# Moving sums, activation steps and prologue pieces in a four-layer state-space kernel

## The chip, the cores and the metric

The kernel runs on one core of a Trainium2 chip, as one program. The metric is its device time in microseconds (us), the median of several runs. All data are float32.

## The reference

Input x is 4 images of 64 x 64 positions (L = 4096) with 128 channels. Layers 0, 1 and 3 are selective state-space blocks, layer 2 is a gated block. Cut to what matters, a state-space block computes, for each of K = 4 directions (rows, columns, and both reversed), DI = 256 channels and N = 16 states:

```python
x_dbl = einsum('bkdl,kcd->bkcl', xs, x_proj_w)          # 8 + 16 + 16 rows
dts, Bs, Cs = split(x_dbl, [R, R + N], axis=2)
delta = softplus(einsum('bkrl,kdr->bkdl', dts, dt_w) + dt_b)
def step(h, t):                                          # over L positions
    x_t, d_t, B_t, C_t = t
    h = exp(d_t[..., None] * A) * h + (d_t * x_t)[..., None] * B_t[:, :, None, :]
    return h, einsum('bkdn,bkn->bkd', h, C_t)
```

Ahead of it stand a layer norm, a projection, a depthwise 3 x 3 convolution and Silu; behind it the four directions are summed, normed, multiplied by Silu of a second projection z, projected and added to the input, and an MLP with Gelu follows.

## The kernel before, in words

**Turns, chunks, periods.** A turn is one state-space layer of one image: 12 turns (`turns`), the images two by two, so that the work between two layers of one image can lie beside the other image's scans. A turn has 32 chunks: four directions by eight chunks of 512 positions. A chunk has 8 periods i = 0 to 7; each handles 4 of the 16 states for one half (128) of the channels. There are 3072 periods. The order of every engine's instructions is written out by hand in the loop over periods (L935 and after); each engine runs its own list in that order, and waits are set by a framework from the tiles.

**A period.** `scan` (L864) is one VectorE scan over 512 positions. Its decay factors `da` come from ScalarE (`decay`, L849: two Exp per call, two calls, made one period ahead). For two of the four states ("side 0") the driving term comes from TensorE in one PSUM tile `dbp` (`pair_db`, L841, issued one period ahead, right after the two scans that free the tile); for the other two ("side 1") VectorE multiplies `dup`, a PSUM copy of delta times x made by ScalarE (`lift`, L857), with `bb`, rows of B that a DMA has spread over the partitions: product `dbv` (L984), one PSUM tile. `lift` copies only in periods 7, 0, 2, 4 and 6, where the half changes. GpSimd multiplies each pair of states with rows of C (`times_c`, L880, tile `hc`); in periods 0, 2, 4, 6 (`PAIRED`) it also adds the two sides. TensorE sums over states by products with the identity into PSUM (`add_up`, L886, tile `yp`): per period two calls for a paired period, four for another. VectorE adds finished sums to `y_sb` (`leave`, L905). `diagonals` (L831) builds on ScalarE the diagonal matrices for `pair_db`; `save` (L874) keeps the last state; `spread` (L816) issues the DMAs of `bb` and `cb` on SyncE's queue.

**The order in a period of before.** ScalarE: decay of the next period, side 0; save; then decay side 1, save, `lift`, `diagonals`. TensorE: the two calls of side 0 of the period before, if that was not paired; `pair_db` for the next period; at the end the two calls of side 1 of the period before. VectorE: two scans, product, scan, product, scan, then in periods 0 and 1 a `leave`.

**Pieces.** The next chunk's preparation is a generator, `prologue` (L761): fetch x; project it to the 40 rows [dt; B; C] (or, for a reversed direction, fetch the rows that the forward one has stored); delta of both halves by projection and Softplus; transposed B (`bt`); `du` = delta times x on GpSimd; `du` transposed (`duT`). `piece(number)` (L945) goes on to its next `yield` at the numbers in `PIECES`; number 2i is behind `pair_db` in period i, 2i + 1 near the period's end. The Softplus piece holds two table loads[...].

**Steps of the work between layers.** Everything else (norms, projections, convolution, Silu, MLP, Gelu) is a list of small steps that `between` makes. `other(number)` (L950) has four slots in each period (0 between the first two scans, 1 behind `piece(2i)`, 2 behind the third scan, 3 at the end) and takes steps from the list's head as their share of the turn has come. `rest` puts empty steps between; `later` sets stores back. The `run` step of `silu` (L419) and `gelu` (L484) are one long activation each, 1024 or 2048 columns, with a table load on either side. In `silu`, `turn` (L424) copies the result transposed into the tile `down` and `store` writes that out; `down` lies in the buffers "cen" and "sq", which `norm` uses too.

**Buffers.** [...] two banks for dbp, one each for dbv, dup, two yp, `misc` (all of the prologue) and `gap` (all the steps). `h` and `hc` have four buffers, `da` three.

Of the kernel before, what the change touches and what calls it, by code (L numbers as in the profile page):

```python
# [13 lines left out]
F32 = mybir.dt.float32  # L14
AF = mybir.ActivationFunctionType
# [10 lines left out]
CH = 512  # L26
NCH = L // CH
RPC = CH // W
P = 128
# [4 lines left out]
PAIRED = (0, 2, 4, 6)  # L34


PIECES = (0, 3, 4, 6, 8, 9, 10, 11, 12, 13)


_VSS = [  # L40
# [24 lines left out]
def vss_stack_kernel(ctx: ExitStack, tc: tile.TileContext, x: bass.AP, weights, out: bass.AP, n_batch=B, layers=(0, 1, 2, 3)):  # L65
# [86 lines left out]
    gap1 = ctx.enter_context(tc.tile_pool(name="gap1", bufs=1))  # L152
    gap2 = ctx.enter_context(tc.tile_pool(name="gap2", bufs=2))
    gap3 = ctx.enter_context(tc.tile_pool(name="gap3", bufs=3))

    def combine(i, psums):

# [39 lines left out]
    def between(e, frm, to, psums):  # L197
# [219 lines left out]
        def silu(c, of_z):  # L417

            def run():  # L419
                part = z.wide[:, 0 if of_z else 2 : 2 if c is None else 4]  # L420
                nc.scalar.activation(part, part, AF.Silu)
# [43 lines left out]
        def mlp(c, store):  # L465
            def fresh():
                z.t = gap1.tile([P, CH], F32, tag="t", name="t")
                return z.t

            norm(lambda: z.res, fresh, v["n2w"], v["n2b"], eps5)  # L470
            for j in range(4):

                def up(j=j):
                    if j == 0:
                        z.wide = gap1.tile([P, 4, CH], F32, tag="wide", name="hid")
                    z.ps = bank()
# [279 lines left out]
    def scans(pool, ring, deep, psum):  # L756
# [4 lines left out]
        def prologue(s):  # L761
# [5 lines left out]
            if s.first:  # L767
                s.dt = pool.tile([R, DI], F32, tag="dt", name="dt_w")
                nc.sync.dma_start(out=s.dt, in_=weights[s.layer][1][:, s.k * DI : (s.k + 1) * DI])
            yield  # L770


            s.xd_d = lane.xd[s.k % 2][s.c]
            s.xd = pool.tile([2 * NX, CH], F32, tag="xd", name="xd")
            if s.back:
                nc.sync.dma_start(out=s.xd[:NX], in_=s.xd_d[1])
                yield
            else:
# [3 lines left out]
                yield  # L782
# [3 lines left out]
            for m in halves:  # L786
                ps = psum.tile([P, CH], F32, tag="misc", name="ps_dt")
                nc.tensor.matmul(ps, s.dt[:, m * P : (m + 1) * P], s.xd[:R], start=True, stop=True)  # L788
                yield
                func = AF.Identity if m == halves[0] else AF.Softplus  # L790
                nc.scalar.activation(s.delta[:, m], ps, func, bias=v["dtb"][:, s.k, m : m + 1])  # L791
            m = halves[0]
            nc.scalar.activation(s.delta[:, m], s.delta[:, m], AF.Softplus)  # L793
            nc.scalar.preload_act_table_set("natural_log_exp_and_others")
            ps = psum.tile([P, 4, NX], F32, tag="misc", name="ps_bt")
            for j in range(4):
                nc.tensor.transpose(ps[:, j, :], s.xd[:NX, j * P : (j + 1) * P], ident[:NX, :NX])
# [66 lines left out]
        def scan(s, i, side, j, da, db):  # L864
            q, m = place(s, i)
            if j == 0:
                s.h[i, side] = deep.tile([P, 2, CH], F32, tag="h", name="h")
            n = CQ * q + 2 * side + j
            init = 0.0 if s.first else s.state[:, m, n : n + 1]
            nc.vector.tensor_tensor_scan(  # L870
                s.h[i, side][:, j, s.step], da[:, j, s.step], db[:, s.step], init, ALU.mult, ALU.add
            )
# [10 lines left out]
            if side == 1 and i in PAIRED:  # L883
                nc.gpsimd.tensor_add(hc, hc, s.hc[i, 0])  # L884

        def add_up(s, i, side):  # L886
            if side == 0 and i in PAIRED:
                return
            q, m = place(s, i)
            start, end = (0, 7) if m == s.flip else (1, 6)  # L890
            opens = i == start and side == int(i in PAIRED)
            if opens:
                setattr(s, f"yp{m}", psum.tile([P, CH], F32, tag=f"yp{m}", name="yp"))
            for j in range(2):
                nc.tensor.matmul(  # L895
                    getattr(s, f"yp{m}"),
                    ident,
                    s.hc[i, side][:, j],
                    start=opens and j == 0,
                    stop=i == end and side == 1 and j == 1,  # L900
                )
            if i == end and side == 1:
                full.append((s, m))

        def leave(s, m):  # L905
            yp, xs = getattr(s, f"yp{m}"), s.xs[:, m]
# [28 lines left out]
        for at, (s, i) in enumerate(periods):  # L935
# [14 lines left out]
            def other(number):  # L950

                gone = at % (8 * per_turn) * 4 + number
                for todo, count, frm, to in segments:
                    while todo and count - len(todo) < count * (gone - frm) / (to - frm):
                        todo.pop(0)()

            da_next = [None, None]
# [6 lines left out]
                save(*before, 1)  # L964
            if spreads:
                spread(*spreads, 0)
            scan(s, i, 0, 0, da[0], s.db[:, :, 0])
# [11 lines left out]
            if then:  # L979
                da_next[1] = decay(*then, 1)  # L980
            save(s, i, 0)
            for j in range(2):
                db = psum.tile([P, CH], F32, tag="dbv", name="dbv")
                nc.vector.tensor_mul(db, s.dup, s.bb[i // 2][:, j])  # L984
                scan(s, i, 1, j, da[1], db)
                if j == 0:
                    other(2)
            times_c(s, i, 1)
            if then:
                if then[1]:  # L990
# [5 lines left out]
                diagonals(s, q, half)  # L996
            elif nxt:
                diagonals(nxt, q - 4, half)
            if i < 2 and full:
                leave(*full.pop(0))  # L1000
            if before:
                add_up(*before, 1)
            piece(2 * i + 1)
            other(3)
            da = da_next
            before = (s, i)
            if then and then[0].turn != s.turn:
                assert not any(todo for todo, *_ in segments)
        save(*before, 1)
        add_up(*before, 0)  # L1010
        add_up(*before, 1)
        while full:
            leave(*full.pop(0))
        for todo, *_ in segments:
# [95 lines left out]
```

## Time and profile before

| what | us |
|---|---|
| median of 3 runs | 23305.67 (23292.7 to 23313.06) |
| the profiled execution, its own time | 23325.13 |
| its span, first to last instruction | 23323.4 |
| busy: VectorE / TensorE / GpSimd / ScalarE | 20362.5 / 20052.7 / 19260.3 / 18075.1 |
| first scan starts at | 165.58 |
| scans (12288) | mean 1.20 to 1.28 each |
| GpSimd products and sums of 128 x 1024 (7680) | 2.36 each |
| products dbv (6144) | 0.69 each |
| table loads | 1.28 each |

The profile is one execution. Its page gives the busy time of each engine, the idle time ahead of groups of instructions and who ended it; its lists of waits name the waiting instruction and line, then the releaser. PE is TensorE, PEld its weight loads, DVE is VectorE, ACT ScalarE, POOL GpSimd, SPq SyncE's queue. A line of a timeline is: start, duration, engine, line, operation, output<-inputs, shapes, count, and in brackets the idle time before it with its releaser. A period takes 7.59 us in the mean (23323.4 less the opening and the end, by 3072), but not the same in all turns: the turns with layer 2's work between (the fourth, fifth, tenth and eleventh) take 2027 to 2037 us, the others 1834 to 1907.

### The profile page before, as it was taken

To read this page: it belongs to the slowest core of one execution; us is meant where nothing else is said; L and a number is where in the kernel's file an instruction comes from. 1 tells how busy PE (TensorE), PEld (TensorE's weight loads), DVE (VectorE), ACT (ScalarE), POOL (GpSimd) and SP (SyncE) were. 2 spreads that over 40 slices of the span, in tenths; PEclk is the share of its full clock that TensorE was granted. 3 is DMA by queue.
4 is the path that set the end of the run, shared out by engine and by line. 5 is a ranking of instruction groups with operands and counts; after the bars stand their busy time and mean duration, and the time that the engine had idled before them with its cause. 6 is when DMAs were issued, how large, how long until landed. Compare 5 with 4: busy or idle time off the path is not lost. (4 is left out here: it accounts for less than half of the span.)

```text
span 23323.4 us, 216855 instructions
## 1 busy us (share of the span) xinstructions
PE 20052.7 (86%) x58234; PEld 10604.8 (45%) x58234; DVE 20362.5 (87%) x20186; ACT 18075.1 (77%) x38870; POOL 19260.3 (83%) x8862
## 2 busy tenths in 40 slices
PE   7888888888888888888888888888888888888887
PEld 3444444444444444444444444444444444444443
DVE  5999899988887888898899899898988878888996
ACT  5788787777777787787788787787877777877886
POOL 5898888888887787888888788888888878878885
PEclk8999999999999999999999999999999999999998
DMA  4444444444334434434533544444443443344332
GB/s 104 147 142 144 131 130 145 131 131 140 125 125 126 130 126 126 135 130 134 139 133 130 139 138 132 134 144 127 132 141 122 126 128 131 123 128 136 131 132 101
DMA packets 2437558, 3060.09 MB, mean 131 GB/s; under 512 B 1753840, under 2 KB 1790064, under 8 KB 2238192
## 3 DMA queue, kind: packets, MB, share of 16 engines
q1 hardware_dynamic: 2436336, 3046.22, 42.1%
q8 instruction: 472, 7.73, 0.1%
q14 instruction: 750, 6.14, 0.1%
HBM read 2784.41 MB, written 261.49 MB: 131 GB/s over the span
## 5 line engine op out<-in xcount | busy, mean ns | idle before, releaser
L882 POOL TENSOR_TENSOR hc<-h,cb 128x1024 f32<-128x1024 f32 x6144 | 14420.4, 2361 | 3675.8 <-DVE h L870 2362.9
L895 PE MATMUL yp<-hc,ident 128*128 128x512 f32 x18432 | 9087.0, 620 | 641.9 <-POOL hc L884 395.2
L854 ACT ACTIVATE da<-delta,w 128x512 f32<-128x512 f32 x12288 | 8158.8, 713 | 1557.2 <-DVE h L870 1532.3
L845 PE MATMUL dbp<-diag,duT 128*128 128x256 f32 x24576 | 6276.1, 400 | 1832.3 <-DVE h L870 1729.2
L870 DVE TENSOR_TENSOR_SCAN h<-da,state,dbp 128x512 f32<-128x512 f32 x5376 | 6564.8, 1259 | 939.5 <-PE dbp L845 757.6
L870 DVE TENSOR_TENSOR_SCAN h<-da,state,dbv 128x512 f32<-128x512 f32 x5376 | 6879.6, 1280 | 477.6 <-ACT da L854 11.1
L845 PEld LDWEIGHTS dbp<-diag,duT 128*128 128x128 f32 x24576 | 4740.1, 198 | 4329.2 <-issue 2850.9
L895 PEld LDWEIGHTS yp<-hc,ident 128*128 128x128 f32 x18432 | 3491.1, 198 | 4992.6 <-issue 3633.6
L984 DVE TENSOR_TENSOR dbv<-dup,bb 128x512 f32<-128x512 f32 x6144 | 4226.0, 688 | 614.2 <-ACT dup L862 400.7
L837 ACT ACTIVATE diag<-ident,bt 128x128 f32<-128x128 f32 x12288 | 3947.5, 401 | 0.2
L884 POOL TENSOR_TENSOR hc<-hc 128x1024 f32<-128x1024 f32 x1536 | 3622.5, 2358 | 120.4
L862 ACT COPY dup<-du 128x512 f32<-128x512 f32 x1920 | 1125.3, 586 | 1267.6 <-DVE dbv L984 1231.8
L402 PE MATMUL gap<-halo,cw 128*128 128x512 f32 x3456 | 1658.6, 605 | 15.6 <-ACT wide L413 6.2
L870 DVE TENSOR_TENSOR_SCAN h<-da,dbp 128x512 f32<-128x512 f32 x768 | 892.5, 1200 | 130.8 <-PE dbp L845 104.1
L870 DVE TENSOR_TENSOR_SCAN h<-da,dbv 128x512 f32<-128x512 f32 x768 | 937.3, 1220 | 79.3 <-ACT da L854 14.1
L805 POOL TENSOR_TENSOR du<-delta,xs 128x512 f32<-128x512 f32 x768 | 978.3, 1274 | 33.7 <-ACT delta L793 33.7
L788 PE MATMUL ps_dt<-xd,dt_w 8*128 8x512 f32 x1536 | 887.2, 658 | 124.9 <-ACT delta L791 73.6
L402 PEld LDWEIGHTS gap<-halo,cw 128*128 128x128 f32 x3456 | 642.1, 192 | 743.8 <-issue 700.7
L878 ACT COPY state<-h 128x2 f32<-128x2 f32 x5376 | 960.9, 179 | 0.0
L413 ACT ACTIVATE wide<-gap,w 128x512 f32<-128x512 f32 x192 | 132.1, 688 | 824.2 <-PE gap L402 824.1
L813 ACT COPY duT<-ps_duT 128x512 f32<-128x512 f32 x768 | 440.0, 573 | 181.3 <-PE ps_duT L811 180.5
L791 ACT ACTIVATE delta<-ps_dt,w 128x512 f32<-128x512 f32 x768 | 524.6, 683 | 37.2 <-PE ps_dt L788 32.6
(121 smaller groups left out, 11443.0 us busy)
## 6 DMA issues: line engine op xcount, KB each, us to landing
cb<-xd_d SPq DMA_DIRECT2D x1536, 1024.0 KB
bb<-xd_d SPq DMA_DIRECT2D x1536, 512.0 KB
xs<-x_row_d SPq DMA_DIRECT2D x192, 512.0 KB
xs<-x_col_d SPq DMA_DIRECT2D x192, 512.0 KB
x_col_d<-down SPq DMA_DIRECT2D x192, 256.0 KB
x_row_d<-wide SPq DMA_DIRECT2D x96, 512.0 KB
y_d<-y_sb SPq DMA_DIRECT2D x96, 512.0 KB
y<-y_d SPq DMA_DIRECT2D x96, 512.0 KB
```

Source lines behind the costliest of these rows:

```text
L402: nc.tensor.matmul(z.ps, z.cw[:, m, t, :], z.halo[c][:, dy : dy + RPC, dx : dx + W], start=(t == 0), stop=(t == 8),)
L805: nc.gpsimd.tensor_mul(s.du[:, m], s.delta[:, m], s.xs[:, m])
L837: nc.scalar.activation(s.diag[q][:, t, :, j], ident, AF.Copy, scale=s.bt[:, t, CQ * q + j : CQ * q + j + 1])
L845: nc.tensor.matmul(s.db[:, t * P : (t + 1) * P, :], s.duT[:, t, m, :], s.diag[q][:, t], start=True, stop=True)
L854: nc.scalar.activation(da[:, j], s.delta[:, m], AF.Exp, scale=s.v["a"][:, s.k, m, n : n + 1])
L862: nc.scalar.copy(s.dup, s.du[:, m])
L870: nc.vector.tensor_tensor_scan(s.h[i, side][:, j, s.step], da[:, j, s.step], db[:, s.step], init, ALU.mult, ALU.add)
L878: nc.scalar.copy(s.state[:, m, n : n + 2].unsqueeze(2), s.h[i, side][:, :, s.end : s.end + 1])
L882: nc.gpsimd.tensor_mul(hc, s.h[i, side], s.cb[i // 2][:, 2 * side : 2 * side + 2, :])
L884: nc.gpsimd.tensor_add(hc, hc, s.hc[i, 0])
L895: nc.tensor.matmul(getattr(s, f"yp{m}"), ident, s.hc[i, side][:, j], start=opens and j == 0, stop=i == end and side == 1 and j == 1,)
L984: nc.vector.tensor_mul(db, s.dup, s.bb[i // 2][:, j])
```

## The change

1. `PIECES` has 14 entries for 10, and the prologue's pieces are cut so that nearly each gives work to one engine. The rows of a reversed direction are fetched with x. B is transposed, and the rows stored, before the second half of delta. The Softplus piece runs at number 9, behind `lift` and `diagonals` of period 4, where it was at number 8, ahead of them; the `du` products run at 10 and 11 (9 and 10 before), the transposes at 12 and 13 (11 and 12), the last copy at 14 (13).
2. `add_up` takes a list of calls. An even period has three, those that are left of the odd period before; an odd one has the two of the paired period before and the first of its own. In odd periods they stand behind the last slot. None stands ahead of `pair_db` in its period any more.
3. `run` of `silu`, and `gelu`, are marked long. At the head of the list, a long step and all behind it are held until slot 3, and in period 4 until slot 3 of period 5.
4. The second product stands ahead of slot 2, not behind it. In period 1, `leave` stands between that product and its scan.
5. Ahead of the first layer, `down` has its own tile with two halves, in the buffer "y".

```diff
-PIECES = (0, 3, 4, 6, 8, 9, 10, 11, 12, 13)
+PIECES = (0, 2, 3, 4, 5, 6, 7, 8, 9, 10, 11, 12, 13, 14)
...
+    long = set()
...
-                z.down = gap1.tile([P, W, RPC], F32, tag=("cen", "sq")[m], name="down")
+                if frm is not None:
+                    z.down = gap1.tile([P, W, RPC], F32, tag=("cen", "sq")[m], name="down")
+                elif m == 0:
+                    z.downs = gap1.tile([P, 2, W, RPC], F32, tag="y", name="down")
+                if frm is None:
+                    z.down = z.downs[:, m]
...
+            long.add(run)
             S.append(run)
...
+            long.add(gelu)
             S.append(gelu)
...
             if s.back:
                 nc.sync.dma_start(out=s.xd[:NX], in_=s.xd_d[1])
-                yield
-            else:
+            yield
+            if not s.back:
                 ps = psum.tile([P, CH], F32, tag="misc", name="ps_x")
...
-                yield
+            yield
+            if not s.back:
                 nc.scalar.copy(s.xd, ps[: 2 * NX])
+            yield
...
+            project(halves[0])
+            yield
+            take(halves[0], AF.Identity)
+            yield
             ps = psum.tile([P, 4, NX], F32, tag="misc", name="ps_bt")
...
             nc.scalar.copy(s.bt, ps[:, :, R : R + N])
+            yield
+            project(halves[1])
+            yield
+            take(halves[1], AF.Softplus)
+            nc.scalar.activation(s.delta[:, halves[0]], s.delta[:, halves[0]], AF.Softplus)
+            nc.scalar.preload_act_table_set("natural_log_exp_and_others")
+            yield
             s.du = pool.tile([P, 2, CH], F32, tag="du", name="du")
...
-        def add_up(s, i, side):
-            if side == 0 and i in PAIRED:
-                return
+        def add_up(s, i, calls):
             q, m = place(s, i)
             start, end = (0, 7) if m == s.flip else (1, 6)
...
+            for call in calls:
+                opens = i == start and call == (2 if i in PAIRED else 0)
+                if opens:
+                    setattr(s, f"yp{m}", psum.tile([P, CH], F32, tag=f"yp{m}", name="yp"))
+                side, j = divmod(call, 2)
+                closes = i == end and call == 3
+                nc.tensor.matmul(getattr(s, f"yp{m}"), ident, s.hc[i, side][:, j], start=opens, stop=closes)
+                if closes:
+                    full.append((s, m))
...
                     while todo and count - len(todo) < count * (gone - frm) / (to - frm):
+                        if (number < 3 or i == 4) and todo[0] in long:
+                            break
                         todo.pop(0)()
...
-            if before:
-                add_up(*before, 0)
             if then:
                 pair_db(*then)
             piece(2 * i)
...
-            for j in range(2):
-                db = psum.tile([P, CH], F32, tag="dbv", name="dbv")
-                nc.vector.tensor_mul(db, s.dup, s.bb[i // 2][:, j])
-                scan(s, i, 1, j, da[1], db)
-                if j == 0:
-                    other(2)
+            scan(s, i, 1, 0, da[1], product(0))
+            db = product(1)
+            other(2)
+            if i == 1 and full:
+                leave(*full.pop(0))
+            scan(s, i, 1, 1, da[1], db)
...
-            if i < 2 and full:
+            if i == 0 and full:
                 leave(*full.pop(0))
-            if before:
-                add_up(*before, 1)
+            if i % 2 == 0 and before:
+                add_up(*before, (1, 2, 3))
             piece(2 * i + 1)
             other(3)
+            if i % 2:
+                add_up(*before, (2, 3))
+                add_up(s, i, (0,))
```

More of the change, by code (lines that the diff above doesn't have):

```diff
@@ L769, in prologue @@
                 nc.sync.dma_start(out=s.dt, in_=weights[s.layer][1][:, s.k * DI : (s.k + 1) * DI])
-            yield
+            ps = None
             s.xd_d = lane.xd[s.k % 2][s.c]
@@ L781, in prologue, with project, take @@
                     nc.tensor.matmul(ps[: 2 * NX], v["xp"][:, s.k % 2, m, :], s.xs[:, m], start=(m == 0), stop=(m == 1))
-                yield
+            yield
+            if not s.back:
                 nc.scalar.copy(s.xd, ps[: 2 * NX])
+            yield
             s.delta = pool.tile([P, 2, CH], F32, tag="delta", name="delta")
             halves = (s.flip, 1 - s.flip)
-            for m in halves:
+            def project(m):
+                nonlocal ps
                 ps = psum.tile([P, CH], F32, tag="misc", name="ps_dt")
                 nc.tensor.matmul(ps, s.dt[:, m * P : (m + 1) * P], s.xd[:R], start=True, stop=True)
-                yield
-                func = AF.Identity if m == halves[0] else AF.Softplus
+            def take(m, func):
                 nc.scalar.activation(s.delta[:, m], ps, func, bias=v["dtb"][:, s.k, m : m + 1])
-            m = halves[0]
-            nc.scalar.activation(s.delta[:, m], s.delta[:, m], AF.Softplus)
-            nc.scalar.preload_act_table_set("natural_log_exp_and_others")
+            project(halves[0])
+            yield
+            take(halves[0], AF.Identity)
+            yield
             ps = psum.tile([P, 4, NX], F32, tag="misc", name="ps_bt")
@@ L884, in times_c @@
                 nc.gpsimd.tensor_add(hc, hc, s.hc[i, 0])
-        def add_up(s, i, side):
-            if side == 0 and i in PAIRED:
-                return
+        def add_up(s, i, calls):
             q, m = place(s, i)
             start, end = (0, 7) if m == s.flip else (1, 6)
-            opens = i == start and side == int(i in PAIRED)
-            if opens:
-                setattr(s, f"yp{m}", psum.tile([P, CH], F32, tag=f"yp{m}", name="yp"))
-            for j in range(2):
[L895 to L903, printed above, removed]
+            for call in calls:
[7 more added lines that the diff above has]
+                    full.append((s, m))
         def leave(s, m):
@@ L966, in scans, with product @@
                 spread(*spreads, 0)
+            def product(j):
+                db = psum.tile([P, CH], F32, tag="dbv", name="dbv")
+                nc.vector.tensor_mul(db, s.dup, s.bb[i // 2][:, j])
+                return db
             scan(s, i, 0, 0, da[0], s.db[:, :, 0])
@@ L981, in scans @@
             save(s, i, 0)
-            for j in range(2):
-                db = psum.tile([P, CH], F32, tag="dbv", name="dbv")
-                nc.vector.tensor_mul(db, s.dup, s.bb[i // 2][:, j])
-                scan(s, i, 1, j, da[1], db)
-                if j == 0:
-                    other(2)
+            scan(s, i, 1, 0, da[1], product(0))
[4 more added lines that the diff above has]
+            scan(s, i, 1, 1, da[1], db)
             times_c(s, i, 1)
@@ L1009, in scans @@
         save(*before, 1)
-        add_up(*before, 0)
-        add_up(*before, 1)
+        add_up(*before, (1, 2, 3))
         while full:
```

## The prediction

> **What bounds the kernel now.** I read the page's engine shares first: VectorE 87%, TensorE 86%, GpSimd 83%, ScalarE 77% busy, no engine full. The scans are a serial chain on VectorE, and from the first scan (165.6 us) to the last period VectorE hardly stops, so I count what it waits for. This is the list of VectorE's waits: who waited, line, releaser, total us, times, longest.
>
> ```profile
> DVE h L870 <- PE dbp L845: 861.7, 417, 10.8
> DVE dbv L984 <- ACT dup L862: 400.7, 205, 5.5
> DVE cen L245 <- ACT gap L242: 262.2, 140, 10.7
> DVE h L870 <- ACT da L854: 131.0, 77, 17.1
> ...
> DVE cen L230 <- DMA x_col_d<-down: 65.1, 2, 32.6
> ```
>
> Two waits lead: a scan waiting for TensorE's product dbp (862 us) and the product dbv waiting for ScalarE's lift dup (401 us). I then sorted these waits in the trace by the period i (0 to 7) that they fall in, four scans being one period. dup: 69, 53, 0, 33, 0, 201, 0, 46 us. dbp: 20, 134, 34, 130, 105, 229, 67, 143: odd periods 636, even 226. Period 5 is worst in both. The timeline of ScalarE ahead of one dup wait in period 5 shows why:
>
> ```profile
> 2846.89 1.28 ACT L791 ACT_TABLE_LOAD   x1
> 2848.19 0.69 ACT L791 ACTIVATE delta<-ps_dt,w 128x512 f32<-128x512 f32 x1
> 2848.77 0.62 ACT L793 ACTIVATE delta<-delta 128x512 f32<-128x512 f32 x1
> 2849.41 1.28 ACT L794 ACT_TABLE_LOAD   x1
> ...
> 2852.14 1.28 ACT L421 ACT_TABLE_LOAD   x1
> 2853.44 1.91 ACT L421 ACTIVATE wide<-wide 128x2048 f32<-128x2048 f32 x1
> 2855.36 1.28 ACT L220 ACT_TABLE_LOAD   x1
> 2856.66 0.59 ACT L862 COPY dup<-du 128x512 f32<-128x512 f32 x1
> ```
>
> The Softplus block (3.87 us) and a Silu with its tables (4.47 us) both stand ahead of the 0.59 us lift. VectorE at that moment:
>
> ```profile
> 2857.28 0.70 DVE L984 TENSOR_TENSOR dbv<-dup,bb 128x512 f32<-128x512 f32 x1 [5.11 <-ACT dup L862]
> ```
>
> Third, TensorE ahead of an odd period: a late pair_db, with VectorE idle 2.46 us for it.
>
> ```profile
> 2622.14 1.88 PE L402 MATMUL gap<-halo,cw 128*128 128x512 f32 x4
> 2623.86 1.88 PE L895 MATMUL yp<-hc,ident 128*128 128x512 f32 x4
> 2625.58 1.89 PE L845 MATMUL dbp<-diag,duT 128*128 128x256 f32 x8
> 2627.60 2.45 DVE L870 TENSOR_TENSOR_SCAN h<-da,state,dbp 128x512 f32<-128x512 f32 x2 [2.46 <-PE dbp L845]
> ```
>
> [...] The trace has the 1283 ns (384 loads, 492.7 us); [...] loads follow their neighbours within 0.1 us, so I use the trace. [...] lift waits behind both tables. So an order is all that this change has to offer, and all that it can spoil.
>
> **The change part by part.** Instruction counts do not change on any engine; what changes is order. The sum is made against the profiled execution, span 23323.4 us in 23325.1 us; the median of the runs is 19.5 us lower.
>
> *Lifts.* After the change no Silu or Gelu is issued between the period's decays and its lift, and the Softplus block comes behind lift and diagonals in period 4, not ahead. I take 0.9 of 401 us: −360. In the 46 chunks with over 1 us of dup wait in period 5, periods 5 to 7 idle 7.4 us in sum, in the others 2.6; the difference, 4.8, exceeds the dup wait itself (4.0), so it isn't given back, and a further 46 × 0.7 us, diagonals queued behind the lift, goes too: −30. Bounds: −200 (period 5 alone) to −430. What is late next on ScalarE is decay: a lift can start about 5.1 us into a period (two scans 2.4, product 0.7, scan 1.28, product 0.7), lift and four diagonals end at 7.0, the Softplus block at 10.9, a Gelu at 11.5, and the next two decays (1.33) at 12.2 or 12.8. Their reader starts at 15.2 (two periods of 7.59). That leaves 3.0 and 2.4 us of cover; other steps' ScalarE work eats some of it, so I charge +30 (0 to +130, the size of today's da wait again).
>
> *Three calls a period.* A summing call is two instructions that issue 0.43 us apart: 0.86 us. Between the pair_db issued in an odd period and the one issued in an even period stand 4 calls today, on the other side 2; afterwards 3 and 3. I compared in the trace the end of each pair_db with the end of VectorE's work before the scan that needs it. Scans of odd periods miss by 696 us in sum; 0.86 us earlier, but never before the scan that frees dbp, gives 471. Scans of even periods miss by 223; 0.86 us later, less TensorE's idle time just before that pair_db, gives 383. Net −65. The one-engine pieces take the wait of TensorE on ScalarE out of its queue (ps_dt on delta 74 us, ps_bt on delta 58), but move a projection and a set of transposes (0.9 and 0.6 us) from odd to even sides: I charge +15 for the two together, so −50. The call that joins an odd period's own end waits for GpSimd's first hc of that period; behind it stand the next slot's steps and pair_db, and behind that the scan. In a late case of the timeline that hc started 6.2 us and ended 8.6 us into its period; pair_db cannot start before the second scan of the next, at 7.6 + 2.4 = 10.0, so 1.4 us cover it: 0. Bounds for the whole: −250 (odd side gains, even side pays nothing) to +200 (the reverse).
>
> *du, the product, leave.* GpSimd gets one du (1.27 us) in each half of period 5, none behind period 4's three big products. Waits of scans on du and hc are 28.7 and 12.6 us; of VectorE's other steps, a quarter now waits behind the second product, 0.7 us of cover each. I take −40 (0 to −80). leave in period 1 is the same 0.88 to 1.06 us of VectorE, earlier: 0. Cover: its yp was closed a period before; if it were late, one wait of today's size (7 us in all).
>
> *xd beside x, its store earlier.* Each of 192 fetches (80 KB) is issued with x, one 0.37 us slot on SyncE's queue ahead of the spreads. Those stand issued a median 17.8 (bb) and 14.4 us (cb) before their first reader: 0. If that cover were gone: 192 × 0.4 = 77 us.
>
> *down in its own buffer.* In the opening, VectorE and ScalarE wait twice for the store of down: the mean is done at 87.9 and its reader starts at 91.9 us, the square waits from 92.6 to 99.2. 2 × 10.6: −21. Its new buffer is y's, which nothing holds there by then.
>
> *What the held-back steps add.* A long step at the head of the list holds all behind it until the period's last slot, from period 4 even until that of 5, seven slots; then they go out together. Counted in the order of the built program: in 7 chunks at the end (last turn, period 5) Silu, gate, projection and VectorE's add share one slot. ScalarE ends about 0.7 us into the next period, GpSimd still has hc and du and reaches the end of gate at 6.0, TensorE's projection at 7, and VectorE stands for about 7.5 us: +52. For 11 Gelus in period 5 three or four of their `down` products are issued right behind, ahead of three summing calls and pair_db. Gelu ends 2.9 into the next period, 4 × 0.86 and 3 × 0.86 end at 8.9, pair_db at 10.9 instead of 7.6: 3.3 us each, 36; the first `down` comes in the same or the next slot for 54 more Gelus, at an estimated 0.3 us each: together +50. Gate and stores of x_col wait for a Silu closer behind them: +30. Bounds for all this: +60 to +400.
>
> Sum: −360 −30 +30 −50 −40 −21 +52 +50 +30 = −339. 23325.1 − 339 = 22986 for such an execution, 22967 at the median's level. I say **22965 us**.
>
> **The rivals.** *Nothing gained:* the dup wait turns into a da wait because ScalarE, 77% busy, is late either way. For it: da already costs 131 us. Against it: ScalarE itself idles 1532 us for buffers of da, so it runs ahead. Given back are, say, 340 of the 390 us: 22967 + 340 = 23307. *More gained:* the pieces and the third call relieve the odd sides by 1.46 us instead of 0.86 (call and transposes); odd misses then fall from 696 to about 355, and even ones stay at 223 because TensorE waits for buffers there (1535 us in sum ahead of even pair_dbs). That is −340 in place of −50: about 22675; half of it, 22820, is more likely. *Slower, by bursts:* 262 long steps are issued in the scans, 79 of them in period 5 with up to seven slots of others behind. Gains are 501 us in the sum; from 501/262 = 1.9 us a long step the change loses. At 2.3 us each: 262 × 2.3 − 501 = +100, 23405. For it: seven of them cost 7.5. Against it: most are followed by rests or by work that only ScalarE does. That the change doesn't do what it says is excluded: the built order shows no Silu or Gelu ahead of a lift, and three calls in every period.
>
> **How the numbers follow.** Forecast 0.60 (own range 22820 to 23120), more gained 0.18, nothing gained 0.10, slower 0.12. Differences under 0.2% (47 us) can't be told from none. The forecast and the larger gain are faster, 0.78; of nothing gained, nearly all is within 0.2%: 0.09; slower takes 0.13 with the rest. The range reaches from 22680, where the larger gain is complete, to 23270: it leaves out the slower case and part of nothing gained.
>
> **What would show it.** Right: dup waits under 60 us in all, none in period 5; odd dbp waits near 470 and even near 380; the waits for down gone from the opening; VectorE idle for a res add about 7.5 us seven times in the last turn. Wrong: da waits over 250 us (ScalarE's cover is used up), dbp waits over 1000 us with TensorE waiting for hid or hc ahead of pair_db (bursts), or waits for bb and cb beyond today's 113 and 396 us (SyncE's queue behind a store).

## The result, and the profile after

The change made the kernel slower: 23471.51 us (median; 23455.11 to 23487.1) against 23304.68 (23292.7 to 23313.06), a ratio of 1.0072, 95% interval 1.0054 to 1.0089. The forecast was 22965, and the range ended at 23270. Medians are compared with the median of the kernel before from the same series; it lies between 23299 and 23316. Turns are counted from 0.

The profiled execution after has a span of 23472.9 us. From its page, the span and the busy times:

```profile
span 23472.9 us, 216388 instructions
...
PE 20087.8 (86%) x58234; PEld 10583.3 (45%) x58234; DVE 20333.9 (87%) x20186; ACT 18081.9 (77%) x38870; POOL 19276.0 (82%) x8862
```

No engine has over 36 us more or less to do than before. The time is in waits. VectorE's list after (who waited, releaser, total us, times, longest):

```profile
DVE h L893 <- PE dbp L868: 921.5, 435, 9.4
DVE dbv L992 <- DMA bb<-xd_d: 254.0, 71, 7.1
DVE h L893 <- ACT da L877: 240.8, 153, 28.8
DVE cen L248 <- ACT gap L245: 237.6, 120, 4.6
DVE res L510 <- PE gap L505: 179.9, 26, 21.9
DVE cen L233 <- PE gap L229: 113.2, 18, 32.2
DVE res L462 <- PE gap L459: 112.6, 15, 13.4
...
DVE dbv L992 <- ACT dup L885: 101.0, 98, 2.7
```

Three lines of the list before, which the prediction does not show:

```profile
DVE dbv L984 <- DMA bb<-xd_d: 112.8, 55, 4.8
DVE res L500 <- PE gap L495: 50.4, 12, 21.4
DVE res L453 <- PE gap L450: 27.8, 7, 13.5
```

The wait for dup did fall, 401 to 101 us, and in period 5 from 201 to 34. But bb rose by 141 us, da by 110, the two sums onto res (the MLP's last, and the one behind the gate's projection) by 130 and 85, dbp by 60. Of the signs that the prediction named for a wrong outcome, one is there: bb far above 113 (and GpSimd's wait for cb, 396 to 556). Another is there in part: TensorE waits for `hid`, the tile that Gelu writes and the `down` products read (94 to 247 us), but dbp stays at 921, under the 1000 named. da missed its mark of 250 by 9.

Where in the program: from the first scan of turn 1 to that of turn 11 the kernel took 19329.8 us before and 19456.9 after (+127), the last turn 1994.3 and 2033.2 (+39), turn 0 7 less; the opening ends 9 earlier.

### The profile page after: what moved, and what is told of

It is laid out like the page before. It is cut to its first block, busy times and chain, and to the rows that moved or that the text cites. A ratio compares the mean times of both kernels' runs of the same rounds, so it can differ in the third digit from the quotient of the medians.

```text
span 23472.9 us, 216388 instructions
## 1 busy us (share of the span) xinstructions
PE 20087.8 (86%) x58234; PEld 10583.3 (45%) x58234; DVE 20333.9 (87%) x20186; ACT 18081.9 (77%) x38870; POOL 19276.0 (82%) x8862
## 2 busy tenths in 40 slices
DMA packets 2437557, 3060.05 MB, mean 130 GB/s; under 512 B 1753841, under 2 KB 1790065, under 8 KB 2238193
## 5 line engine op out<-in xcount | busy, mean ns | idle before, releaser
L920 PE MATMUL yp<-hc,ident 128*128 128x512 f32 x18432 | 8822.5, 611 | 500.7 <-POOL hc L907 329.4
L834 PE MATMUL ps_duT<-ident,du 128*128 128x128 f32 x3072 | 488.5, 284 | 267.6 <-ACT duT L836 227.3
L505 PE MATMUL gap<-hid,pw 128*128 128x512 f32 x768 | 428.9, 682 | 261.7 <-ACT hid L494 246.5
```

Of the source, the lines that this page charges most:

```text
L920: nc.tensor.matmul(getattr(s, f"yp{m}"), ident, s.hc[i, side][:, j], start=opens, stop=closes)
```

## The experiments

Two theories were open. A: holding Silu and Gelu loses the time, because what is kept behind them comes out too close. B: the three calls, or the fourteen pieces, lose it by making dbp late.

### One part at a time

`e1_no_hold`, the changed kernel less this:

```diff
-                        if (number < 3 or i == 4) and todo[0] in long:
-                            break
```

> The changed kernel without the holding of long steps: Silu and Gelu go out in whatever slot their share of the turn has come. Theory A (the holding loses the time, since what is kept behind a long step goes out in a burst: TensorE then waits for Gelu, VectorE for the projections behind it, and SyncE's queue is late with bb): the bursts' waits go, 'res' waits from 292 back to about 80, bb from 254 to about 115, TensorE's wait for hid from 246 to about 95; dup waits come back in part, from 101 to 200 to 250. Time about 23120, faster than before. Theory B (the three calls or the fourteen pieces lose it, by making the dbp of even periods late, 498 against 223): even dbp stays near 500, and the time stays near 23450.

`e1_hold_only`, the kernel before with this and the two `long.add` alone:

> The kernel before with the holding of long steps alone; calls, pieces, the products' order and down as before. Theory A: the bursts are all there and little pays for them: dup falls only by the part that Silu and Gelu cause (401 to about 250), bb and res waits rise as in the changed kernel (254 and 230); time about 23550. Theory B: the holding is worth its part of dup and costs little; time about 23150.

`e1_pieces_only`, the kernel before with the new `prologue` and `PIECES`:

> The kernel before with the fourteen pieces alone (Softplus behind lift and diagonals of period 4, fetch beside x). Theory A: a gain, since period 5 alone held 201 us of dup waits and its diagonals queue behind the lift: about 23120. Theory B: the projection and transposes that move to the even sides make dbp there late (223 to 350 or more): no gain, about 23300.

`e1_calls_only`, the kernel before with the new `add_up`, its calls, and the new places of the second product and `leave`:

> The kernel before with three summing calls a period and the second product ahead of slot 2 alone. The recorded step said a gain of some 50 to 90 us (odd dbp 696 to 471, even 223 to 383). Theory A: odd near 470, even 300 to 400, time about 23240. Theory B: even near 500, and the time about 23400, slower than before.

`e4_calls_pure`, the same, but the product and `leave` stay where they were:

> The kernel before with the three summing calls a period alone; the second product and leave stay where they were. With these moved too it took 23158. If the calls carry the gain: 23150 to 23190, dbp of odd periods near 420 by the page's names. If the earlier product carries a part: 23230 or more.

| kernel | us | of before, us | ratio (95%) |
|---|---|---|---|
| e1_no_hold | 23247.1 | 23316.01 | 0.9972 (0.9961 to 0.9983) |
| e1_hold_only | 23560.84 | 23316.01 | 1.0105 (1.0091 to 1.0119) |
| e1_pieces_only | 23411.42 | 23316.01 | 1.0041 (1.0028 to 1.0054) |
| e1_calls_only | 23157.95 | 23316.01 | 0.9933 (0.9919 to 0.9946) |
| e4_calls_pure | 23216.18 | 23314.28 | 0.9961 (0.9948 to 0.9975) |

The parts add up: calls and product −158, pieces +95, holding +245, and the opening's 9 us give +173, where the whole gave +167. Theory A holds for the largest part. B falls for the calls, which gained more than either theory said, and holds for the pieces, which lose where A expected a gain and B none: two parts out of three lose. A's time for `e1_hold_only` (23550) was met; its 23120 for `e1_no_hold` was not.

### The holding: Silu or Gelu

Each keeps one of the two `long.add` lines.

> The changed kernel with only Silu held; Gelu goes out when due. Holding both took 23471, none 23247, so 224 us are to be split. If the stores behind Silu and the last turn's res waits (120 us more with holding) make the loss: about 23400 to 23430, bb near 250 and the last turn 60 us longer than without holding. If it is what stands behind Gelu (TensorE's wait for hid, 246 against 95 us): about 23290, bb near 115.

> The changed kernel with only Gelu held; Silu goes out when due. The counterpart: about 23290 if Silu's stores and gates make the loss, with bb back near 115 and res of the last turn near 50; about 23400 if Gelu's followers make it, with the wait for hid still near 246.

23385.77 (1.0034, 1.0022 to 1.0047) and 23346.77 (1.0015, 1.0009 to 1.0022): 139 and 100 above the kernel without holding, so both lose. Each expectation had one of the two make the loss, and neither was right. The waits part as expected: bb is 257 with Silu alone and 118 with Gelu alone, TensorE's wait for hid 95 and 246.

What such a loss looks like: the changed kernel in the last turn, at the end of period 5, where a Silu and all that was kept behind it share one slot.

```profile
22962.13 1.28 ACT L424 ACT_TABLE_LOAD   x1
...
22963.43 1.06 ACT L424 ACTIVATE wide<-wide 128x1024 f32<-128x1024 f32 x1
22964.50 1.28 ACT L223 ACT_TABLE_LOAD   x1
22964.56 2.34 POOL L454 TENSOR_TENSOR y<-y,wide 128x1024 f32<-128x1024 f32 x1 [0.72 <-ACT wide L424]
...
22966.96 3.78 PE L459 MATMUL gap<-y,pw 128*128 128x512 f32 x4 [10.62 <-POOL y L454]
...
22970.78 0.69 DVE L462 TENSOR_TENSOR res<-res,gap 128x512 f32<-128x512 f32 x1 [12.57 <-PE gap L459]
```

Silu, gate, projection, sum, each waiting for the one before; TensorE has stood 10.6 us and VectorE 12.6, with scans behind it. And a Gelu in turn 3, whose four `down` products (eight instructions) went out right behind it:

```profile
5821.05 1.91 ACT L494 ACTIVATE hid<-hid 128x2048 f32<-128x2048 f32 x1
...
5823.01 5.37 PE L505 MATMUL gap<-hid,pw 128*128 128x512 f32 x8 [7.49 <-ACT hid L494]
...
5828.42 0.75 DVE L510 SCALAR_TENSOR_TENSOR res<-gap,w,res 128x512 f32<-128x512 f32 x1 [10.02 <-PE gap L505]
```

### The holding: rate or distance

`e2_hold_drip`: in turns 1 to 10 a long step ends its slot, and a slot takes at most two steps of the backlog.

```diff
+                        if 0 < s.turn < 11 and taken == 2:
+                            break
...
+                        if 0 < s.turn < 11 and step in long:
+                            break
```

> The changed kernel, holding as before, but in turns 1 to 10 a long step is the last of its slot, and of what has piled up behind it at most two steps go out in a slot. Theory A (the burst costs, not the holding): dup stays near 100, the waits for res (121 us in these turns), for bb (254) and for Gelu on TensorE fall towards 30, 150 and 100; dbp falls with them; time 23250 to 23330. Rival (it is the holding, since everything behind the long step is late whatever its rate): time stays within 50 us of 23470.

23429.46 (1.0048, 1.0035 to 1.0061), 42 less only: by the marks set, the rival's result. A lower rate alone helps little. The wait for hid fell to 125, but bb stayed at 266 and res at 285. In the built order the stores of the transposed image still stood one scan behind their `turn` in 116 of 192 cases (two or more behind it in 175 without holding).

That pointed to the empty steps. `rest` keeps followers apart by empty entries in the list; a backlog takes entries without regard to their being empty, so the distance goes. In the built order the first `down` stands 0 or 1 scans behind Gelu in 2 of 96 cases without holding and in 65 with it; stores 0 or 1 behind their `turn` in 17 and 78 of 192; a gate has no scan between it and its Silu in 1 and 14 of 96. `e4_hold_rests` holds as the changed kernel does, but in turns 1 to 10 alone and only while over 40 steps of the list are left, and gives the distances back:

```diff
+                        held = 0 < s.turn < 11 and len(todo) > 40
+                        if held and todo[0] in long and (number < 3 or i == 4):
+                            break
+                        if held and taken == (1 if slow[0] else 3):
+                            break
...
+                        if held and step in long:
+                            slow[0] = 7
+                            break
+                    slow[0] = max(0, slow[0] - 1)
```

> The changed kernel holding in turns 1 to 10 alone, a long step the last of its slot, and after it for six slots at most one step a slot, an empty one counted like any other, then at most three. In the built order its followers get back the distance of the kernel before (first down at least 2 scans behind Gelu, add at least 5 behind Silu, stores 2 behind their turn). Without holding 23247, with it 23471. If the holding loses because the backlog eats the empty steps that kept followers apart: TensorE's wait for hid back from 246 to about 100, res of turns 1 to 10 from 121 to about 40, bb from 254 to about 130, dup still near 130: time 23080 to 23200. If it loses because everything behind a long step is late and crowds into the periods after, whatever its distances: 23380 or more.

23174.82 (0.9939, 0.9927 to 0.9952): 297 less than with plain holding, 72 less than without any. By the profiled executions:

| | turns 1 to 10 | last turn |
|---|---|---|
| no holding | 19314.7 | 1965.6 |
| holding | 19456.9 | 2033.2 |
| holding, distances kept (none in the last turn) | 19231.4 | 1960.1 |

So in turns 1 to 10 holding with its distances is worth −83 us, and the lost distances cost 225; the last turn adds 68. These are single executions. The one without holding lies 15 us above the median of its runs, the one with distances 7 below, so that −60 is a better estimate than −83. Which part of the hold loses, the one to the period's end or the longer one from period 4 to 5, was not tried by itself. TensorE's wait for Gelu before, in the changed kernel, then here:

```profile
PE gap L495 <- ACT hid L485: 93.9, 42, 4.0
```

```profile
PE gap L505 <- ACT hid L494: 246.5, 70, 9.2
```

```profile
PE gap L505 <- ACT hid L494: 54.0, 42, 4.0
```

bb is back at 114 and cb at 308. The expectation missed on res: 164 us of it are left in turns 1 to 10 (121 before the edit), in many small waits.

### The holding: the stores

SyncE's queue in the changed kernel, behind a Silu: start, duration, operation.

```profile
2406.29 0.37 SPq L438 DMA_DIRECT2D x_col_d<-down  x1
2406.76 4.49 SPq L844 DMA_DIRECT2D bb<-xd_d  x1
2411.29 0.57 SPq L444 DMA_DIRECT2D x_row_d<-wide  x1
2411.97 0.54 SPq L844 DMA_DIRECT2D cb<-xd_d  x1
2412.62 1.03 SPq L438 DMA_DIRECT2D x_col_d<-down  x1
2414.08 8.49 SPq L844 DMA_DIRECT2D bb<-xd_d  x1
```

The issue of bb takes 0.32 us at the median, and here 4.5 and 8.5 behind a store of x_col, which writes 32 bytes at a time. Four kernels store in runs of 2 KB. They leave out the transposed order; the number and order of all instructions stay:

```diff
-                to_col = lane.x_col[:, m].rearrange("p (w h) -> p w h", h=H)
-                nc.sync.dma_start(out=to_col[:, :, c * RPC : (c + 1) * RPC], in_=z.down)
+                to_col = lane.x_col[:, m, cols(c)].rearrange("p (w h) -> p w h", w=W)
+                nc.sync.dma_start(out=to_col, in_=z.down)
```

> The changed kernel, with the transposed image stored in runs of 2 KB in place of runs of 32 bytes, at other positions, so that the column directions compute on wrongly ordered data; bytes and order of all instructions stay. If the bb waits of 254 us come from the two stores of x_col that now stand close together ahead of bb on SyncE's queue, they fall to about 115 and the time to about 23330. If bb is late only because it stands behind steps that wait for ScalarE, they stay above 220 and the time within 30 us of 23470.

> The kernel before with the transposed image stored in runs of 2 KB (at other positions: the column directions compute on wrongly ordered data). In the changed kernel this edit took off 277 us (23471 to 23194). If the 32-byte stores hurt both kernels alike, it takes off 250 to 280 here too: about 23040. If it is the holding that makes them collide with bb and cb, it takes off only what bb (113) and cb cost today, 100 to 150: about 23180, and the rest, 130 to 170 us, is the holding's.

> The changed kernel without holding and with stores in runs of 2 KB (at other positions: the column directions compute on wrongly ordered data). The pair with holding is 23471 and 23194. If lost distance mostly brings the short stores together and in front of bb and cb, the holding costs little once they are gone: about 23150 here, 45 us below the pair with holding. If it mostly puts products, gates and sums too close to their activation: about 23010, holding still costs 180 or more.

> The holding that keeps the distances (23175), with stores in runs of 2 KB. If its 297 us over the changed kernel came mostly by spacing the stores: about 23110, some 60 us below it. If they came from the other followers: about 22930, some 245 us below it, as much as in the kernel before.

| us, medians | runs of 32 bytes | runs of 2 KB | less |
|---|---|---|---|
| before | 23310.15 | 23068.22 (e3_before_runs; 0.9897, 0.9884 to 0.9911) | 242 |
| changed | 23471.51 | 23194.18 (e2_col_runs; 0.9946, 0.9933 to 0.9958) | 277 |
| changed, no holding | 23247.1 | 23081.99 (e5_no_hold_runs; 0.9905, 0.9889 to 0.9922) | 165 |
| changed, distances kept | 23174.82 | 23024.23 (e5_hold_rests_runs; 0.9883, 0.9868 to 0.9897) | 151 |

`e2_col_runs` alone would have misled: it undid 277 us, more than the whole loss, but the kernel before gains 242 by the same edit. Holding costs 224 us with short stores and 112 without (23194 against 23082); the distances are worth 297 and 170. In turns 1 to 10 holding with distances is then worth −48, not −83. So about half of the holding's loss came through the short stores ahead of bb and cb, and half stays without them, with products, gates and sums. (Taken against the kernel before of its own series each, holding costs 236 and 100.) That the wait for bb rose by 141 us doesn't say that it cost 141.

Nor were more issues held up. Issues of bb that took over 2 us are 57 before, 60 in the changed kernel and 60 without holding, with 399, 408 and 419 us in sum. They come later: bb is issued at the head of an odd period, for the product of the next, and of these long issues 4, 35 and 1 began more than 4 us into that period.

### The pieces

`e2_softplus_late`, the kernel before, not recut, with its pieces from Softplus on one number later:

```diff
-PIECES = (0, 3, 4, 6, 8, 9, 10, 11, 12, 13)
+PIECES = (0, 3, 4, 6, 9, 10, 11, 12, 13, 14)
```

> The kernel before, its ten pieces not recut, only those from Softplus on one number later (9, behind lift and diagonals of period 4). If the place is what costs: dup falls by about 120, da of period 6 rises by 100 or more, dbp of period 0 by 90; time about 23400, as with the fourteen pieces (23411). If the recut is what costs: only the gain of dup is seen, time about 23180.

`e2_pieces_early`, no holding, recut, Softplus and what follows one number earlier:

```diff
-PIECES = (0, 2, 3, 4, 5, 6, 7, 8, 9, 10, 11, 12, 13, 14)
+PIECES = (0, 2, 3, 4, 5, 6, 7, 8, 9, 10, 11, 12, 13)
...
             take(halves[0], AF.Identity)
-            yield
```

> The changed kernel without holding, and with the Softplus piece and all behind it one number earlier (8, ahead of lift, as in the kernel before); the take of the first half shares a piece with the transposes of B to make room. Its neighbour without this edit took 23247 us. If the place of the Softplus piece is what the pieces lose by (decays of period 6 queue behind it, the copies of duT come half a period late for period 0), the da waits of period 6 fall from about 130 to about 25, dbp of period 0 from 130 to 45, dup of period 5 rises from 69 to about 210: time about 23150. If it is the recut with its moved projection and transposes, the time stays near 23247.

The late ten pieces took 23632.14 (1.0137, 1.0123 to 1.0151), 320 more than before: the place costs, and more so uncut: the transposes of B stand behind Softplus in that piece, Softplus now behind lift and diagonals, and TensorE waits for delta there (776 us against 58). The early recut took 23131.76 (0.9921, 0.9907 to 0.9934), 115 less than the same kernel with Softplus at 9; da fell from 323 to 162, dbp of period 0 from 112 to 37, and dup of period 5 rose from 69 to 186. So number 9 is the wrong place for Softplus and what follows it. The cut itself costs nothing at 8: `e1_calls_only`, which lacks it and the new `down`, took 23158.

Why, from `e1_pieces_only`, ScalarE around a Softplus piece:

```profile
3134.10 1.28 ACT L850 ACTIVATE diag<-ident,bt 128x128 f32<-128x128 f32 x4
3135.40 1.28 ACT L795 ACT_TABLE_LOAD   x1
3136.69 0.69 ACT L795 ACTIVATE delta<-ps_dt,w 128x512 f32<-128x512 f32 x1
3137.28 0.62 ACT L813 ACTIVATE delta<-delta 128x512 f32<-128x512 f32 x1
3137.92 1.28 ACT L814 ACT_TABLE_LOAD   x1
3139.21 1.28 ACT L485 ACT_TABLE_LOAD   x1
3140.50 1.91 ACT L485 ACTIVATE hid<-hid 128x2048 f32<-128x2048 f32 x1
3142.43 1.28 ACT L220 ACT_TABLE_LOAD   x1
3143.72 1.33 ACT L867 ACTIVATE da<-delta,w 128x512 f32<-128x512 f32 x2
```

and VectorE, in period 6:

```profile
3144.53 2.45 DVE L883 TENSOR_TENSOR_SCAN h<-da,state,dbp 128x512 f32<-128x512 f32 x2 [6.19 <-ACT da L867]
```

Softplus block and Gelu, 8.3 us back to back, no longer stand ahead of a lift but ahead of the next decays. This list needs care, though. In another period 6 of this kernel:

```profile
5118.24 1.33 ACT L867 ACTIVATE da<-delta,w 128x512 f32<-128x512 f32 x2
...
5120.87 1.89 PE L858 MATMUL dbp<-diag,duT 128*128 128x256 f32 x8
...
5122.89 2.45 DVE L883 TENSOR_TENSOR_SCAN h<-da,state,dbp 128x512 f32<-128x512 f32 x2 [1.65 <-ACT da L867]
```

The scan is put down to da, which was ready at 5119.57; it began when dbp ended, at 5122.76. I therefore gave each late first scan of a period to the later of its two inputs. From before to the pieces alone: da 79 to 201 us, of which period 6 24 to 129; dbp of odd periods about 725 to 547, of even ones about 242 to 388, period 0 alone 22 to 121. The last is the copies of duT, which came half a period later (TensorE's wait for them before the second transposes: 65 to 328 us).

What stood between the decays of a late first scan and the decays ahead of them? With the pieces alone, in period 6, it was the Softplus block and a long activation in 17 cases (74 us) and the Softplus block alone in 41 (55 us). In the changed kernel the holding keeps these two apart. There it was the Softplus block alone in 41 cases of period 6 (54 us), and a held Silu or Gelu in 31 cases of period 7 (41 us; under 1 us before). One of the latter, with two copies of `down` right behind the Silu:

```profile
5346.86 1.28 ACT L424 ACT_TABLE_LOAD   x1
5348.15 1.92 ACT L424 ACTIVATE wide<-wide 128x2048 f32<-128x2048 f32 x1
5350.09 1.28 ACT L223 ACT_TABLE_LOAD   x1
5351.38 2.06 ACT L434 COPY down<-wide 128x512 f32<-128x512 f32 x2
5353.35 1.33 ACT L877 ACTIVATE da<-delta,w 128x512 f32<-128x512 f32 x2
...
5354.50 2.45 DVE L893 TENSOR_TENSOR_SCAN h<-da,state,dbp 128x512 f32<-128x512 f32 x2 [3.10 <-ACT da L877]
```

### The fastest versions

`e3_early_actq` is `e2_pieces_early` with the stores of x_col issued by ScalarE:

```diff
-                nc.sync.dma_start(out=to_col[:, :, c * RPC : (c + 1) * RPC], in_=z.down)
+                nc.scalar.dma_start(out=to_col[:, :, c * RPC : (c + 1) * RPC], in_=z.down)
```

> The kernel without holding and with the Softplus piece at number 8 (23132 us), its 192 stores of the transposed image issued by ScalarE in place of SyncE. If bb and cb are late because they stand behind these stores in SyncE's queue: bb from 95 to below 40, cb from about 400 to below 200, and 100 to 150 us less, less up to 71 us of ScalarE's issue time (192 by 0.37): 23000 to 23080. If the transfer engines themselves are full with short runs: bb and cb stay, time 23130 to 23200.

22958.37 (0.9852, 0.9837 to 0.9867): 173 less than on SyncE's queue, and below both kernels. bb waits fell from 95 to 1 us, cb from 414 to 43. The two queues, at such a place:

```profile
2392.64 0.37 ACTq L438 DMA_DIRECT2D x_col_d<-down  x1
2397.20 0.32 SPq L843 DMA_DIRECT2D bb<-xd_d  x1
...
2398.44 2.12 ACTq L438 DMA_DIRECT2D x_col_d<-down  x1
2401.02 0.32 SPq L843 DMA_DIRECT2D cb<-xd_d  x1
```

bb and cb are issued in 0.32 us again, though the same short runs are under way. Now the stores themselves are held up: 65 of the 192 took over 2 us to issue from ScalarE (up to 6.5; on SyncE's queue none took over 2). The wait for dup rose from 396 to 447 us; whether the one causes the other was not tried.

`e4_early_actq_hold` adds the holding that keeps distances:

> The fastest so far (no holding, Softplus piece at 8, stores of the transposed image issued by ScalarE: 22958) with the holding that keeps the distances, in turns 1 to 10. If that holding is worth its part of dup (447, of which Silu and Gelu cause some 200): 22800 to 22900. If lateness itself costs: 23000 to 23100.

23039.19 (0.9882, 0.9869 to 0.9896), 81 more, as expected if lateness itself costs. dup fell from 447 to 324, but res rose from 87 to 250; the turns with layer 2's work between took 100 us more, the other turns from 1 to 10 21 less. On the base with Softplus at 9 the same holding gained 72. Why it depends on the base stays open.

## Why the prediction was wrong, point by point

- *What the held-back steps add, +132: the step that failed most.* Holding cost 245 alone and 224 in the whole, net of what it took off dup (237 and 212 us of wait). By the prediction's own rates, one us of time for one of wait, it should have gained about 80 in the whole (an estimate: 212 less 132). The mechanism was the recorded rival's, "slower, by bursts", and its 23405 was the nearest figure. That nearness is partly luck: it set 603 us of holding against 501 of gains, where holding and pieces lost 340 and the rest gained 165. The argument against it, that most long steps "are followed by rests", is the error: the rests are entries of the very list that is held, and the backlog eats them. I had counted the followers that end up in the long step's own slot, and priced most others at 0.3 us.
- *The seven chunks of the last turn, 7.5 us each.* The place and the count were right; it was 12.6 us in six of them and 9.4 in the seventh. Six waits of 6.2 to 6.5 us for the sum behind Gelu, in period 2 of these chunks, were not counted at all. The working let ScalarE end 0.7 us into the next period; but the Softplus block, decays and diagonals stand ahead, so in the case shown Silu's table load begins 3.9 us and its activation ends 6.3 us into it (the last scan before ended at 22958.21).
- *Lifts, −390.* dup fell by 300 of 401, under the 360 expected, and the rest did not follow. For the holding's part, with distances kept, 141 us less dup (313 to 172) bought 60 to 83 us, 48 with the stores out of the way. So a microsecond of wait taken away was not a microsecond of time, as the sum had it. For Softplus's part it bought nothing: the pieces lose 95.
- *da, +30 (0 to +130).* The cover of 3.0 and 2.4 us, worked out for the Softplus block or a long activation alone, did not hold in the whole even for one of them, in 41 and 31 cases as counted above; with the pieces alone both also met. What used the cover up in each case stays open, but for the `down` copies in the case shown. In the page's lists da rose by 110 in the whole, inside the bounds, and by 166 with the pieces alone. The rival "nothing gained" had this mechanism.
- *Nothing was charged for the copies of duT*, which the change's list moved to 13 and 14 with the rest: about 100 us of dbp in period 0. "Of a step that is moved, everything it issues counts" was not carried to the end of the generator.
- *Three calls, −50: right in sign and mechanism, too small.* −98 alone (the working had −65 without the pieces' part). By the count of the prediction odd scans missed by 425 (471 expected) and even ones by 352 (383) in `e4_calls_pure`. In the whole, odd came out at 470 and even at 498: the even side's extra is the pieces' and the holding's.
- *du, product, leave, −40.* The product and leave are worth 58 (23216 less 23158, with their own references 2 us apart). The scans' waits for du fell from 28.7 to 13.4 in the whole.
- *down, −21.* The wait of 65 us for the store went, but TensorE's mean became late in the opening (36 to 93 us), and the first scan starts 9.4 us earlier. *xd beside x, 0* was not tried by itself; no wait for xd is among the longer ones.

The measured parts (calls −98, product −58, pieces +95, holding +245, opening −9) sum to +175. A slip without effect: the 384 table loads of 492.7 us are those of one line of the kernel; all lines together have 1297.

For the blocks that were moved, the order of ScalarE's list decided. In the profile before, all 31872 of its decays, state copies, lifts and diagonals run in the order that the loop writes, as do VectorE's 18432 scans and products: moving a block only changed who is behind it. In `e1_pieces_only` the decays at 3143.72 began only when the Softplus block and Gelu, 8.3 us, were through.

## What to carry to other kernels

When a step is held back in a list with built-in gaps, the gaps are held with it and are consumed by the catching up; give the followers their distance anew, or price each of them as waiting for the held step in full. When a block moves within an engine's list, follow it to the next reader of everything behind it, together with the worst neighbour that can join it, and to the end of its own chain. And an edit that undoes a loss proves its cause only if the kernel before doesn't gain the same by it.

## What the runs showed of the hardware

A store of 256 KB in runs of 32 bytes is issued in 0.37 us at the median on SyncE's queue, but an issue of bb right behind one took up to 10.6 us, and 59 of the 60 issues of bb over 2 us stand right behind one (changed kernel). Issues of bb over 2 us are 64 in `e2_pieces_early`, one in `e3_early_actq` and one in `e3_before_runs`. The page counts 1753841 packets under 512 bytes in the changed kernel, 180976 in `e3_before_runs`. With the stores issued by ScalarE the kernel took 173 us (0.7%) less: SyncE's issues of bb and cb took 1711 us in `e2_pieces_early` and 1080 in `e3_early_actq`, and the waits for both fell (95 to 1 us, 414 to 43). No run here shows why an issue behind such a store takes longer.
